# End of a graph layer's second step: the third last tile's sum leaves its accumulator amid the last tile's search for maxima, and the proofs' test stands later

## The chip, the cores and the metric

The kernel runs on one core of one Trainium2 chip. The metric is the device time of one execution in microseconds (us); the median of three runs before the change is 1416.24 us. Engines are called by the names of the profile: PE is TensorE's matmul, PEld its weight load, DVE is VectorE, ACT is ScalarE, POOL is GpSimd, SP is SyncE, which issues most of the DMAs.

## The reference

A graph layer with attention is computed on 3327 nodes of 256 features, in two steps (STEPS = 2). Cut to what matters:

```
def _top_p_attention(X, W1, W2, W3):
    q = X @ W1.T @ W2.T
    k = X @ W3.T
    probs = softmax(q @ k.T, axis=-1)
    idx = argsort(-probs, axis=-1)
    sp = take_along_axis(probs, idx, axis=-1)
    cs = cumsum(sp, axis=-1)
    keep_sorted = cs - sp < 0.9
    mask = zeros(probs.shape, bool).at[rows, idx].set(keep_sorted)
    A = probs * mask
    return A / maximum(A.sum(-1, keepdims=True), 1e-12)

h = maximum(layernorm(x), 0)
R = adj + eye;  R = R / R.sum(-1, keepdims=True)
Z = 0;  Xf = Xa = h
for n in range(2):
    A = _top_p_attention(Xa, W1, W2, W3)
    Xf = R @ Xf
    Xa = A @ Xa
    Z = Z + Xf @ U1[n].T + Xa @ U2[n].T
y = h + Z
out = x + (y - mean(y)) / sqrt(var(y) + 1e-5) * ln_g + ln_b
```

For each row of attention only the largest probabilities are kept, until their sum reaches 0.9. The kernel doesn't sort: it guesses a threshold near the cut, and then finds the exact cut among the values just below the guess.

## The kernel before

The 3327 rows make 26 tiles of 128 rows (NT = 26, numbered 0 to 25). A tile of attention is a block `e` of 128 rows by 3328 columns, in float32. In each of the two steps a tile passes through these stages:

- `weights` (L582): logits on PE, exponentials on ACT, into `e`.
- `measured_twice` (L669, in the second step): passes of ACT over `e` and small operations on DVE and POOL, which guess the threshold.
- `settle` (L725): the exact cut, all on DVE but for one product on POOL. L731 writes the values below the guess into `w`; twenty MAX8 (L736) take the eight largest of each of twenty segments; rounds of MAX8 and MATCH_REPLACE8 (L743, L745) order these candidates; a cumulative sum (L750) gives the cut; L765 masks `e` with it (for the last tile L762 does this in two pieces, of 1024 and of 2304 columns, so that the first columns are ready earlier); L766 makes the factor `ra` that divides by the row's sum; L769 notes one value more for the proof.
- `Sums` (L797): `turn` transposes `e` on PE, four blocks of 128 columns at a time (a part; seven parts to a tile, the last of two blocks), into a buffer `pt` of PSUM, and ACT copies it to `eT` (L812). `sum` multiplies these with the rows of the layer (L824) into the accumulator `pa`. There are two buffers `pt`, three `eT`, and one `pa`. Parts are turned two parts ahead of the sum, so the last parts of one tile's sum stand between turns of the next tile's parts.
- `finish` (L934, in the second step), in pieces that are called one by one: L935 on DVE takes the sum out of `pa`, scales it with `ra` and adds it to `s`; `spread_of` (L458, L459 on DVE) gives mean and variance; the third piece asks SP for the rows `xr` of x (L940, one buffer) and makes 1/sqrt (L465, L466) and `nm` (L943) on POOL; the fourth adds `bet` (L945, POOL) and normalises, by L950 on ACT and L951, L952 on POOL, or by L947, L948 on DVE for the last tile; the fifth stores the rows (L955).

`proof` (L957) ends the second step: `prove(1)` is twelve small DVE instructions (L777 to L788) that test whether all the cuts found are exact, and the second piece adds up the outcome over the partitions with a matmul (`pf`, L961) and writes it to `flag` (L962). All engines read `flag` at the end (L1193); if it were set, a slow search would follow.

The order of the work is written out by hand. In each step a loop over i (L1115) begins the stages of its tiles as generators and then runs through seven slots k (PARTS = 7). In a slot it turns parts, then advances one generator by one piece for each letter of a string, and then sums one part. The strings are in PLAN (L1103) and, for the last rounds of the second step, in LAST (L1106). The letters concerned: `d` is a piece of `settle` of tile i, `n` of `measured` of the tile, `c` what was left of the settling of the tile before, `f` of `finish` of the tile summed last, `s` of the diffusion (`pr`, L911, L1086), `v` of `proof`. In the second step the sum lags four slots (LATE), so that in round i the sum of tile i-2 ends in slot 3 and that of tile i-1 begins in slot 4; `settle` has seven pieces, of which the first ends after L732, the second after ten MAX8, the third after twenty, and the sixth before L769. What is left of a string's generators at the end of a round is run out there (L1174).

The last lines (L1182 to L1185) tie the instructions of PE, ACT, DVE and POOL to the order of this text, each engine for itself. SP's order isn't tied.

Of the kernel before, what the change touches and what calls it, by code (L numbers as in the profile page):

```python
# [22 lines left out]
NT = (N + P - 1) // P  # L23
# [321 lines left out]
def guess_graph_layer(ctx, tc, x, adj, w1t, w2t, w3t, u1t, u2t, ln_g, ln_b, out, flag):  # L345
# [236 lines left out]
    def weights(step, t, live, known=True):  # L582

        r = dict(Z=rec[:, step, 3, t : t + 1])
        qT, r["ms"] = yield from project(step, t, law=known and not step)
        if known and step:
            r["ms"] = law_of(t)
        yield
        r["ms"] = r["ms"] or early.get(t)
        r["e"] = e = es[(2, 3, 0, 1, 4, 5)[t % 6] if step else t % 4]  # L590
        r["za"] = za = small.tile([P, CUT + 1], F32, tag="za", name="za")
        live[step, t] = r
        w = HALF * P
        wd = w // CUT
        for n in range(CUT):
            c = n * wd
            pl = ps_l.tile([P, 2, 512], F32, tag="pl", name="pl")
            for a in range(2):
                p = slice(a * DA, (a + 1) * DA)
                PE.matmul(pl[:, a, :wd], qT[p, :],  # L600
                          keys_of(step, a).rearrange("p a b -> p (a b)")[:, c : c + wd],
                          start=True, stop=True)
            if n < CUT - 1:
                S.activation(e.rearrange("p (a n) -> p a n", a=2)[:, :, c : c + wd], pl[:, :, :wd],  # L604
                             AF.Exp, accum_out=za[:, n : n + 1])
                yield
            else:
                S.activation(e.rearrange("p (a n) -> p a n", a=2)[:, :, c : w - 1], pl[:, :, : wd - 1],
                             AF.Exp, accum_out=za[:, n : n + 1])
                S.activation(e[:, w - 1 : w], pl[:, 0, wd - 1 : wd], AF.Exp, accum_out=za[:, n + 1 :])  # L610
# [108 lines left out]
    def measured(step, r):  # L719
        return measured_twice(r) if step else measured_once(r)  # L720
# [52 lines left out]
    def prove(step):  # L773
        v8, t, tn, Z = (rec[:, step, k, :] for k in range(4))
        ok = small.tile([P, NT], F32, tag="cum", name="ok", bufs=1)
        o2 = small.tile([P, NT], F32, tag="dr", name="o2", bufs=1)
        V.tensor_tensor(ok, v8, t, ALU.is_lt)  # L777
        V.tensor_tensor(o2, tn, t, ALU.is_lt)
        V.tensor_tensor(ok, ok, o2, ALU.mult)
        for a, c, op in ((tn, 0.0, ALU.is_gt), (t, 0.5 * BIG, ALU.is_lt),  # L780
                         (Z, 1.0e-30, ALU.is_gt), (Z, BIG, ALU.is_lt)):
            V.scalar_tensor_tensor(ok, a, c, ok, op, ALU.mult)
        V.tensor_scalar(ok, ok, 0.5, None, ALU.is_lt)
        n = N - (NT - 1) * P
        f = small.tile([P, 1], F32, tag="f", name="f")
        V.tensor_reduce(f, ok[:, : NT - 1], AX.X, ALU.add)
        V.tensor_tensor(fl, fl, f, ALU.add)
        V.tensor_tensor(fl[:n], fl[:n], ok[:n, NT - 1 :], ALU.add)  # L788
        if step == 0:
            V.tensor_scalar(ok, lists[:, :, LIST - 1], 0.0, None, ALU.is_gt)  # L790
            V.scalar_tensor_tensor(ok, ends, float(P), ok, ALU.is_gt, ALU.add)
            V.tensor_reduce(f, ok, AX.X, ALU.add)
            V.tensor_tensor(fl, fl, f, ALU.add)
# [125 lines left out]
    def first_end(t):  # L919
        aT = transposed(live.pop(("r", t)))  # L920
        yield
        pz = ps_r.tile([P, 2 * D], F32, tag="pr", name="pz")
        for c in range(ND):
            PE.matmul(pz, aT[:, c, :], u2[:, c].rearrange("p n d -> p (n d)"), start=c == 0, stop=c == ND - 1)
        S.copy(xw[:, t, :], pz[:, D:])
        sv = row.tile([P, D], F32, tag="sv", name="sv", bufs=2)
        S.copy(sv, pz[:, :D])
        G.tensor_tensor(sv, sv, x0[:, t, :], ALU.add)
        nc.sync.dma_start(sx[t], sv)
        yield  # L930
        yield from prep(aT, t)
# [25 lines left out]
    def proof():  # L957
        prove(1)
        yield
        pf = ps_t.tile([P, 4, P], F32, tag="pt", name="pf")  # L960
        PE.matmul(pf[:1, 0, :1], fl, ones, start=True, stop=True)  # L961
        V.tensor_copy(flag, pf[:1, 0, :1])  # L962

    live, ohs, acs, xgs, done, early = {}, {}, {}, {}, [], {}
    none = iter(())

    def run(work, n=99):
        for _ in range(n):
            next(work, None)
# [133 lines left out]
    PLAN = (("mdsssa", "mdsssa", "edawwp", "msda", "mpdea", "gdawwq", "emdgq"),  # L1103
            ("llcmss", "lnms", "lwwnfd", "lcmdsssg", "fmswqdf", "llmdf", "lmwfd"))

    LAST = {NT - 1: ("cfss", "cn", "ndddddd", "sss", "fsf", "f", "f"), NT: ("cf", "v", "", "", "ff", "f", "fv")}  # L1106
    LATE = (1, 4)
    trace, begin = nc.cur_bb.bb.instructions, len(nc.cur_bb.bb.instructions)
    work = dict(m=none, d=none, f=none)
    later = {}  # L1110
    ordered = []
    for step in range(2):
        sums = Sums(step, live, xw if step else x0, AHEAD[step])

        for i in range(-1, NT + 2):  # L1115
            if step == 0 and i == NT - 3:
                begun = [weights(1, t, live, False) for t in range(3)]
            if step == 1 and i == -1:
                ordered.append(len(trace))
            if step == 1 and i == -1:  # L1120
                run(begun[0])
                prove(0)
                for e in es[4:]:
                    G.memset(e[:, N:NP], 0.0)
            work.update(
                n=work["m"],
                c=work["d"],
                d=settle(step, i, live[step, i]) if valid(i) else none,
                m=measured(step, live[step, i + 1]) if valid(i + 1) else none,
                s=spread(step, i - 2 + 2 * step) if valid(i - 2 + 2 * step) else none,  # L1130
                w=later.pop((step, i + 2), none),
                e=first_end(i - 2) if step == 0 and valid(i - 2) else none,
                a=lister if step == 0 and i else none,
                p=packed(i + 1) if step == 0 and i >= 0 and valid(i + 1) else none,
                g=none if not valid(i + 2 * step) else refetch(i + 2) if step else gathered(i),
                b=none, q=none, v=proof() if step and i == NT else none,
                l=laws(range(3, NT)) if step and i == -1 else none,
            )
            if i >= 0 and valid(i + 3):
                later[step, i + 3] = weights(step, i + 3, live)  # L1140
                work["q"] = itertools.islice(later[step, i + 3], 2 - step)
            if step == 0 and i >= NT - 2 and i < NT + 1:

                work["w"] = itertools.islice(begun[i - NT + 2], CUT - 1)
            if step == 0 and i >= NT - 3 and i < NT:
                work["q"] = itertools.islice(begun[i - NT + 3], 1)
            if i == -1:
                work["w"] = begun[1] if step == 0 else itertools.chain(begun[1], begun[2])
            if step == 0 and i == 0:
                work["w"] = begun[2]  # L1150
            if step == 0 and i < 1:
                work["b"] = itertools.islice(product, MADE if i else NT)
            if step == 1 and i == -1:
                work["g"] = itertools.chain(refetch(0), refetch(1))
            for k in range(PARTS):
                g = PARTS * (i - 1) + k - LATE[step]
                summing = valid(g // PARTS)
                if summing and step:
                    sums.turn(g, min(i, NT - 1))
                for c in "bb" + (LAST.get(i, PLAN[1]) if step else PLAN[0])[k]:  # L1160
                    next(work[c], None)
                if summing and not step:
                    sums.turn(g, min(i, NT - 1))
                if summing:
                    ended = sums.sum(g)
                    if ended and step == 0:
                        live["r", ended[0]] = ended[1]
                    elif ended:
                        work["f"] = finish(ended[0], live.pop(("f", ended[0])), *ended[1])
            if step == 1 and i == -1:  # L1170
                run(work["m"])
            if step == 0 and i == -1:
                G.memset(es[2][:, N:NP], 0.0)
            for c in "lcnwqsepgb" if step else "dmwqsepgb":  # L1174
                run(work[c])
            if step == 0 and i == NT:
                moments(1, gsum)
                for t in range(3):
                    live[1, t]["ms"] = returned(project(1, t, queries=False))
# [50 lines left out]
```

## Time and profile before

| what | us |
|---|---|
| median of three runs | 1416.24 (1415.47 to 1416.34) |
| the profiled execution | 1414.41 |
| its span on the core | 1412.7 |
| what lies around the span in that execution | 1.7 |
| PE busy | 1275.6 (90% of the span) |
| DVE busy | 1220.8 (86%) |
| ACT busy | 1105.4 (78%) |
| POOL busy | 983.1 (70%) |
| last DVE instruction (L948) starts | 1402.98 |
| last store issued (L955) | 1403.49 |

Times inside the span are counted from its start. The span was cut by the profiler into 40 slices of 35 us. In all but the first, the last and those around the middle (where the second step begins) PE and DVE are busy in 90% or more of a slice: there the engines work on several tiles at once. Near the end no tiles are left to fill the gaps. The change lies there, in the last 60 us, and a share of busy time over the whole span says nothing on it; the stretch has to be read by itself. In the timelines an "x8" beside L824 counts records: a matmul in float32 leaves two, so it is four matmuls, one part of a sum.

### The profile page before, as it was taken

Reading aid. Unit: us, or ns where it says so; the run is one execution under the profiler, and the core shown is the slowest. Engines: PE = TensorE matmul, PEld = TensorE weight load, DVE = VectorE, ACT = ScalarE, POOL = GpSimd, SP = SyncE. Lnnn points to the kernel's source line nnn. Section 1 sums busy time; section 2 is a strip of 40 time slices with the busy share of each in tenths; the row PEclk is TensorE's granted clock in tenths of the full one; section 3 lists DMA queues with packets and bytes.
Section 4 is the critical chain, followed back from the end, with each engine's and each line's share of the span. In section 5 each row is a group of like instructions: output and inputs, shape, how many; then the busy total and the mean of one; then the engine's idle time right before and its main releaser. Section 6 shows DMA issues by size and latency. Waiting matters only on the chain.

```text
span 1412.7 us, 22245 instructions
## 1 busy us (share of the span) xinstructions
PE 1275.6 (90%) x6495; PEld 980.1 (69%) x6495; DVE 1220.8 (86%) x3727; ACT 1105.4 (78%) x2423; POOL 983.1 (70%) x1348
## 2 busy tenths in 40 slices
PE   6898999999999999999998479999999999999846
PEld 5545777777777777778786257777777777777745
DVE  6879999999999999998853689999999999999980
ACT  5467887878778787888835689999999999999811
POOL 6214777678667676778853768888888888888721
PEclk9999999999999999999999589999999999999978
DMA  8884454444545454423331211312222122221100
GB/s 273 266 254 127 135 150 130 137 139 141 144 128 147 128 143 144 132 82 91 88 97 49 71 44 54 90 57 79 76 59 87 55 85 59 77 83 53 57 8 22
DMA packets 91203, 149.78 MB, mean 106 GB/s; under 512 B 15265, under 2 KB 58656, under 8 KB 91072
## 3 DMA queue, kind: packets, MB, share of 16 engines
q1 hardware_dynamic: 73616, 105.37, 23.7%
q0 software_dynamic: 16640, 42.69, 11.9%
q8 instruction: 54, 0.88, 0.3%
q14 instruction: 77, 0.63, 0.1%
q10 hardware_dynamic: 816, 0.20, 0.1%
HBM read 120.93 MB, written 27.28 MB: 105 GB/s over the span
## 4 chain that ended last, share of the span: by engine, by line
DVE 51%; PE 25%; ACT 17%; POOL 3%; issue 3%; DMA 1%; SPq 0%; DVEq 0%; POOLq 0%; ACTq 0%
ACT ja L633 11%; PE pa L824 10%; DVE e L765 10%; DVE cand L736 7%; DVE w L731 6%; DVE fm L846 5%; PE pl L600 4%; DVE bb L743 4%; DVE cand L745 4%; PE pt L810 3%; PE pz L988 2%; DVE x L765 2%; ACT eT L812 2%; PE pr L911 1%; ACT e L604 1%
## 5 line engine op out<-in xcount | busy, mean ns | idle before, releaser
L824 PE MATMUL pa<-xw,eT 128*128 128x256 f32 x1352 | 331.1, 387 | 18.6 <-DVE s L935 18.4
L633 ACT ACTIVATE ja<-e,g 128x3328 uint8<-128x3328 f32 x106 | 325.9, 3074 | 0.1
L824 PE MATMUL pa<-x,eT 128*128 128x256 f32 x1352 | 323.7, 381 | 0.0
L824 PEld LDWEIGHTS pa<-xw,eT 128*128 128x128 f32 x1352 | 249.6, 191 | 79.6 <-issue 27.1
L812 ACT COPY eT<-pt 128x512 f32<-128x512 f32 (+1 forms) x364 | 202.1, 556 | 92.9 <-PE pt L810 92.8
L824 PEld LDWEIGHTS pa<-x,eT 128*128 128x128 f32 x1352 | 244.1, 191 | 25.7
L736 DVE MAX8 cand<-w 128x8 f32<-128x168 f32 (+1 forms) x1040 | 251.1, 317 | 0.0
L810 PE MATMUL pt<-ident,e 128*128 128x128 f32 x1144 | 180.6, 278 | 57.9 <-DVE e L765 39.1
L894 POOL DMA_INDIRECT ac<-in_adj,index x130 | 130.2, 1002 | 133.1 <-DVE ms L538 94.9
L903 POOL DMA_INDIRECT xg<-bx,index x130 | 192.4, 1480 | 41.3 <-issue 28.9
L810 PEld LDWEIGHTS pt<-ident,e 128*128 128x128 f32 x1144 | 140.8, 144 | 104.7 <-issue 48.8
L731 DVE SCALAR_TENSOR_TENSOR w<-e,g 128x3328 f32<-128x3328 f32 x44 | 168.9, 3838 | 0.7
L903 POOL DMA_INDIRECT xg<-vx,index x130 | 130.8, 1007 | 45.6 <-issue 33.0
L765 DVE SCALAR_TENSOR_TENSOR e<-e,rec 128x3328 f32<-128x3328 f32 x40 | 156.3, 3907 | 0.7
L911 PE MATMUL pr<-xg,ac 128*128 128x257 f32 (+1 forms) x520 | 139.1, 391 | 11.4 <-DVE s L1086 11.2
L604 ACT ACTIVATE e<-pl 128x832 f32<-128x832 f32 x132 | 112.9, 859 | 36.1 <-PE pl L600 36.0
L911 PEld LDWEIGHTS pr<-xg,ac 128*128 128x128 f32 x520 | 93.9, 195 | 24.9 <-DVE s L1086 11.4
L951 POOL TENSOR_TENSOR s<-s,gam 128x256 f32<-128x256 f32 x25 | 92.5, 3699 | 8.5 <-ACT s L950 8.5
L743 DVE MAX8 bb<-cand 128x8 f32<-128x160 f32 x286 | 92.8, 324 | 6.4
L600 PE MATMUL pl<-after,qT 64*128 64x416 f32 x416 | 96.7, 559 | 0.6 <-ACT qT L528 0.6
L767 POOL TENSOR_TENSOR cum<-dr,bb 128x48 f32<-128x48 f32 x26 | 84.8, 3262 | 15.1 <-DVE rec L755 14.9
L600 PE MATMUL pl<-both,qT 64*128 64x416 f32 x416 | 90.7, 539 | 0.9 <-DVE both L1006 0.9
(259 smaller groups left out, 2197.3 us busy)
## 6 DMA issues: line engine op xcount, KB each, us to landing
at<-in_adj SPq DMA_DIRECT2D x102, 256.0 KB, 3.0
cx<-ac SPq DMA_DIRECT2D x26, 384.0 KB, 2.3
ac<-cx SPq DMA_DIRECT2D x26, 384.0 KB, 3.1
wide<-in_adj SPq DMA_DIRECT2D x10, 832.0 KB, 4.3
e<-in_adj SPq DMA_DIRECT2D x8, 832.0 KB, 5.9
bx<-e SPq DMA_DIRECT2D x26, 128.5 KB, 2.2
own<-bx SPq DMA_DIRECT2D x26, 128.5 KB, 2.9
x<-in_x SPq DMA_DIRECT2D x13, 256.0 KB, 4.7
```

The source lines that it names most:

```text
L600: PE.matmul(pl[:, a, :wd], qT[p, :], keys_of(step, a).rearrange("p a b -> p (a b)")[:, c : c + wd], start=True, stop=True)
L633: S.activation(ja, e, f, bias=guess, scale=sign, accum_out=total)
L731: V.scalar_tensor_tensor(w, e, col(16), e, ALU.is_lt, ALU.mult, accum_out=d2)
L736: V.max(cand[:, 8 * s : 8 * s + 8], w[:, s * SEG : min(NP, (s + 1) * SEG)])
L743: V.max(b8, cand)
L765: V.scalar_tensor_tensor(e, e, at(1), e, ALU.is_ge, ALU.mult, accum_out=ra)
L810: PE.transpose(pt[:, j, :], e[:, (j0 + j) * P : (j0 + j + 1) * P], ident)
L812: S.copy(eT[:, :w, :], pt[:, :w, :])
L824: PE.matmul(self.pa, eT[:, c - 4 * k, :], self.xa[:, j, :], start=c == 0, stop=c == NT - 1)
L894: G.indirect_dma_start(out=ac[:, k, :], out_offset=None, in_=rows, in_offset=bass.IndirectOffsetOnAxis(ap=index[:, t, k : k + 1], axis=0), ...
L903: G.indirect_dma_start(out=xg[:, k, :w], out_offset=None, in_=rows, in_offset=bass.IndirectOffsetOnAxis(ap=index[:, t, k : k + 1], axis=0))
L911: PE.matmul(pr[:, :w], ac[:, k, :], own if k == KT - 1 else xg[:, k, :w], start=k == 0, stop=k == KT - 1)
```

## The change

The strings for the last rounds of the second step are written anew, and there is one more of them (i = NT + 1 = 27, a round that had none of its own). A line is touched so that a proof begun in round 26 is kept for round 27.

```
-    LAST = {NT - 1: ("cfss", "cn", "ndddddd", "sss", "fsf", "f", "f"), NT: ("cf", "v", "", "", "ff", "f", "fv")}
+    LAST = {NT - 1: ("cfss", "cn", "ndd", "sss", "fddddsf", "f", "f"), NT: ("cf", "", "", "", "ff", "fv", "f"),
+            NT + 1: ("fv", "f", "", "", "f", "f", "f")}
...
-                b=none, q=none, v=proof() if step and i == NT else none,
+                b=none, q=none, v=proof() if step and i == NT else work.get("v", none),
```

In round 25, slot 2, two pieces of tile 25's settling remain (up to the tenth MAX8) where there were six; the other four stand in slot 4, behind the first `f`, which is L935 of tile 23. So on DVE L935 of tile 23 moves from behind L766 of tile 25 to between its tenth and eleventh MAX8. The second `f` (L458 and L459 of tile 23) stays where it was, behind L766, and so do the later pieces. On DVE the twelve instructions of `prove(1)` move from ahead of L935 of tile 24 to behind its L459. On PE the matmul `pf` moves behind one further part of tile 25's sum and one further turn. The order on ACT and POOL is the same in both kernels. On SP the reading of `flag` stood between the load of `xr` for tile 24 and the store of tile 24, and stands behind that store and the load of `xr` for tile 25. No instruction is added or taken away on any engine.

## The prediction

> **What bounds the kernel now.** I read the page first: DVE carries 51% of the chain that ended last and PE 25%, but these are means over 1412.7 us, and the change touches only the last 60 us. So I asked for the chain of waits from 1350 us on (columns: start, us, engine, tile, line).
>
> ```profile
> 1354.72 4.67 DVE cand L736 x20
> 1364.85 3.85 DVE e L762 x4
> 1369.51 3.78 PE pa L824 x8
> 1386.11 1.99 PE pa L824 x8
> 1395.13 4.33 PE pa L824 x20
> ```
>
> Until 1369 us the end is set by DVE's settling of tile 25, the last one; after that by PE, which makes two whole sums (tiles 24 and 25) back to back. Why PE starts so late is in the list of waits over 1350 to 1412.7 us (total, times, longest):
>
> ```profile
> PE pa L824 <- DVE s L935: 15.1, 1, 15.1
> ```
>
> PE's timeline shows the place (start, duration; one matmul is two records, so x8 is four blocks of the sum; in brackets the idle time before).
>
> ```profile
> 1353.78 0.60 PE L911 MATMUL pr<-own,ac 128*128 128x256 f32 x2
> 1369.51 3.78 PE L824 MATMUL pa<-xw,eT 128*128 128x256 f32 x8 [15.13 <-DVE s L935]
> 1373.90 1.89 PE L824 MATMUL pa<-xw,eT 128*128 128x256 f32 x8
> 1381.90 0.60 PE L810 MATMUL pt<-ident,e 128*128 128x128 f32 x4
> 1386.11 1.99 PE L824 MATMUL pa<-xw,eT 128*128 128x256 f32 x8
> ```
>
> The sum of tile 23 was complete by 1353.5 us, but `pa` has one buffer, and it is emptied by L935 on DVE, whose turn comes only after all of tile 25's settling. DVE's timeline:
>
> ```profile
> 1354.64 4.75 DVE L736 MAX8 cand<-w 128x8 f32<-128x168 f32 x20
> 1364.85 1.28 DVE L762 SCALAR_TENSOR_TENSOR e<-e,rec 128x1024 f32<-128x1024 f32 x1
> 1368.91 0.16 DVE L766 RECIPROCAL ra<-ra 128x1 f32<-128x1 f32 x1
> 1368.99 0.47 DVE L935 SCALAR_TENSOR_TENSOR s<-pa,ra,s 128x256 f32<-128x256 f32 x1
> 1369.49 0.43 DVE L458 BATCH_NORM_STATS2 st<-s 128x6 f32<-128x256 f32 x1
> 1369.95 0.18 DVE L459 BATCH_NORM_AGGREGATE mv<-st 128x2 f32<-128x6 f32 x1
> ```
>
> L935 wanted nothing but its place in DVE's order for 15 us. Last the order on ScalarE, which becomes decisive below: the finishing step L950 of tile 23 stands between the fifth and the sixth copy of tile 24's turned blocks (the copy at 1374.15 us is the fourth).
>
> ```profile
> 1376.32 0.59 ACT L812 COPY eT<-pt 128x512 f32<-128x512 f32 x1 [1.58 <-PE pt L810]
> 1376.80 0.60 ACT L950 ACTIVATE s<-s,nm,rstd 128x256 f32<-128x256 f32 x1
> 1378.48 0.58 ACT L812 COPY eT<-pt 128x512 f32<-128x512 f32 x1 [1.08 <-PE pt L810]
> ```
>
> And TensorE's granted clock by stretches (third last number of a line):
>
> ```profile
> 1354.00:1369.50 15.50, 0.38 (x2) 0.00 (x0) 14.80 (x52) 0.58 (x1) 1.30 (x1) 0.59 0.00 0
> 1369.50:1374.00 4.50, 4.49 (x13) 3.64 (x14) 3.58 (x15) 0.00 (x0) 1.75 (x4) 0.52 0.00 0
> 1374.00:1386.00 12.00, 11.97 (x67) 10.31 (x65) 0.43 (x1) 3.80 (x7) 1.45 (x2) 1.00 0.07 22
> ```
>
> In stretches of half a microsecond the clock falls to 0.50 at 1356.7, 2.3 us after PE's last work, and is back at 1.00 at 1373.7. So the first 4.2 us of tile 24's sum ran at half speed.
>
> **What the Trainium skill says.** "TensorE: Matmul & The Clock Gate", section "Part 1: The HAM clock gate", says that PE falls to half clock after about an idle window of 3.4 us and needs a busy window of about 3.4 us to come back, the windows free-running. The trace agrees on the two speeds and the grid (from 1356.7 to 1373.7 is 17.0 us, five times 3.4), and shows that a window need not be wholly idle: the one that ended at 1356.7 still held 1.1 us of work, a third. "PSUM — Partial Sum Buffer", section "Engine vs sequencer instructions", says that ScalarE, VectorE and GpSimdE queues are strictly first in, first out, and that matmuls keep program order. The trace agrees: L935 sat behind the settling for 15 us. The sums below rest on both.
>
> **The change part by part.**
>
> 1. L935 of tile 23 goes from behind L766 to the middle of the twenty MAX8. The first ten take 2.36 us from start to next (1331.80 to 1334.16, where the kernel already does this for the tile before), so it starts at 1354.64 + 2.36 = 1357.0 and ends at 1357.47. PE's sum was ready 3.5 us earlier: no wait is added for the ten MAX8 and the settling behind it. It displaces them by 0.39 us (the same L935 in the search before, 1334.16 to 1334.54, and L1086, 1334.91 to 1335.30, are such steps). PE starts tile 24's sum at 1357.5 instead of 1369.5: 12.0 us earlier, after an idle of 3.1 us.
>
> 2. How far PE gets. Up to the first turn of tile 25 stand five parts at 1.73 us (1376.06 to 1377.79), three turns at 0.44 (1375.62 to 1376.06) and the short one at 0.22: 8.65 + 1.32 + 0.22 = 10.2 us at full clock. Before it took 1369.51 to 1381.90 = 12.4 us, so the cold start cost 2.2. At full clock PE is there at 1367.7, and tile 25's first masked columns are ready at 1366.14 + 0.39 = 1366.5.
>
> 3. What is late next. That turn needs a `pt` buffer (there are two), the one that the copy of tile 24's sixth part frees. In ScalarE's order, which the change leaves as it was, this copy stands behind L950 of tile 23. L950 needs `nm` from GpSimd, and that needs L458 and L459 on DVE, which the change leaves behind the whole settling. L766 begins at 1368.91 + 0.39 = 1369.30, L458 at 1369.38 (0.08 after it, as L935 did), L459 ends 0.64 later, as before (1369.49 to 1370.13), at 1370.02; GpSimd's three steps took 1370.13 to 1371.48 = 1.35, so `nm` is there at 1371.37; a hop of 0.07 (as 1377.40 to 1377.47, L950 to L951); L950 holds the queue 0.48 (1376.32 to 1376.80 is such a step), the copy takes 0.58: 1372.51. PE turns tile 25's first part at about 1372.56 against 1381.90, which is 9.34 us earlier. PE stands still for up to 4.9 us before it.
>
> 4. The clock after this standstill. A PE idle for 4.9 us falls to half clock in nearly every position of the 3.4 us grid and stays there until a busy window ends, so half of the cold time is lost: at least half a window, 1.7, at most 3.4 if nearly two windows pass. If PE already went cold in the gap of 3.1 us, its first parts run longer, at the expense of the standstill only, which may then be too short to count: loss 0. I take 1.8 (the page's window halved, little more; the trace's own case was 2.2), ends 0 and 3.4.
>
> 5. What follows is the old tail: L935 of tile 24 between the sums, sum of tile 25, L935 to L948, last store; 1386.11 to 1412.7, moved as a block. L950 of tile 24 had 3.2 us to spare (`nm` at 1388.06, L950 at 1391.28) and keeps them, as its chain starts at the same L935. xr for tile 24 is loaded behind tile 23's store: L951 and L952 end near 1373.7, the load is issued at about 1374.1, and L945 wants it after tile 24's L459, at about 1380.
>
> 6. The proof: twelve DVE instructions, 1370.69 to 1373.46 = 2.8 us, go behind tile 24's L459, where DVE was idle (4.13 us before L962). They end near 1382.2; `pf`, moved one part later on PE, comes at 1393.03 - 7.5 = 1385.5, so 3.3 us hide it; without this cover the excess would stand on PE. The matmul costs 0.12 on PE in either place (1390.64 to 1390.76). On SP the flag's load moves behind tile 24's store and the next xr load; only the last store, 10 us later, stands behind it: nothing.
>
> Sum: 9.34 - 1.8 = 7.5 us off the span of 1412.7, so 1405.2. What lies around the span (1414.41 - 1412.7 = 1.7) stays. The timed median is 1.8 above the profiled run; the same gain gives 1416.24 - 7.5 = 1408.7.
>
> **Rivals.** (a) The clock is kept, or PE goes cold in the first gap and has recovered by 1372.6: gain 9.3, 1406.9. For it: gaps of 2.5 us (before 1334.68) left the clock alone; against: 4.9 us is long, and the gap of 6.1 us before 811 us was followed by half clock. (b) L950 doesn't bind, because its chain runs earlier than I read it: PE goes through at 1367.7, gain 14.2, 1402.0. Against: the order on DVE and ScalarE is fixed by hand, and L458 keeps its place. (c) The wait only moves: something in the tail that I hold to be covered (the xr load, the proof, tile 24's L950) is late by over 6.5 us; then less than 2.8 us, 0.2%, remains, about what a measurement can tell from no change: 1415. Against: the margins of 3 us and more above. (d) Slower: PE, restarted at 1372.6, doesn't recover its clock and runs the rest of both sums, 17.5 us at full clock (1381.90 to 1399.45), at half. That costs 17.5 against 9.3 gained: 1424.4. It decides from 18.7 us of cold running on; the longest cold work seen, with gaps in it, is 795.9 to 803.6, 7.7 us.
>
> **How the numbers follow.** Forecast 0.62, (a) 0.24, (b) 0.05, (c) 0.05, (d) 0.04. Faster: 0.62 + 0.24 + 0.05 = 0.91; same 0.05; slower 0.04. The range takes (a) with 0.7 us for the unknown grid position in the runs before (their own cold loss may be 1.7 to 3.4 where the profiled one had 2.2), and the largest cold loss (gain 5.9, 1410.3) with a little over: 1406.2 to 1410.6.
>
> **What would show it.** L935 of tile 23 at 1357.0 amid the MAX8; PE's idle split in two, about 3 us ended by L935 and up to 5 us ended by ScalarE's copy behind L950; the first turn of tile 25 near 1372.6; the clock at 0.50 for 3 to 5 us after it; L935 of tile 24 near 1378, the last sum's end near 1392, the span near 1405. The prediction is wrong if L950 of tile 23 runs before 1370 us (then b), if PE's second gap is missing, or if the last sum's start moves by less than 5 us.

## The result, and the profile after

| | before | after |
|---|---|---|
| median, us | 1415.86 (4 runs, 1414.3 to 1416.34) | 1406.62 (4 runs, 1406.2 to 1408.79) |
| ratio after / before | | 0.9938, 95% interval 0.9926 to 0.9949 |
| profiled execution, us | 1414.41 | 1408.79 |
| its span, us | 1412.7 | 1407.1 |
| tile 25's L731 starts, us | 1350.78 | 1352.80 |
| first MAX8 of tile 25's search, us | 1354.64 | 1356.66 |
| from that MAX8 to the end of the span, us | 58.06 | 50.44 |

The change makes the kernel faster by 9.2 us, or 7.2 to 10.5 by the interval. The two profiled spans differ by less, 5.6 us, because in the execution profiled after the change everything ahead of the changed place came 2.0 us late. The order of instructions there is the same in both kernels, so the place for a comparison is the stretch from tile 25's search on: it is 7.62 us shorter.

The list of waits from 1345 us on, kernel after (total, times, longest):

```profile
ACT s L950 <- POOL nm L943: 8.6, 1, 8.6
...
PE pt L810 <- ACT eT L812: 4.6, 1, 4.6
...
PE pa L824 <- DVE s L935: 3.1, 1, 3.1
```

The one wait of 15.1 us has split in two. The accumulator now holds PE for 3.1 us. Then, five parts of the sum later, a copy on ScalarE holds it for 4.6, and that copy was held by L950, which itself waited 8.6 us for `nm`. DVE's timeline shows the moved instruction and what stayed behind:

```profile
1356.66 2.44 DVE L736 MAX8 cand<-w 128x8 f32<-128x168 f32 x10
1359.01 0.47 DVE L935 SCALAR_TENSOR_TENSOR s<-pa,ra,s 128x256 f32<-128x256 f32 x1
1359.40 2.40 DVE L736 MAX8 cand<-w 128x8 f32<-128x168 f32 x10
...
1371.33 0.16 DVE L766 RECIPROCAL ra<-ra 128x1 f32<-128x1 f32 x1
1371.41 0.41 DVE L458 BATCH_NORM_STATS2 st<-s 128x6 f32<-128x256 f32 x1
1371.86 0.18 DVE L459 BATCH_NORM_AGGREGATE mv<-st 128x2 f32<-128x6 f32 x1
```

The statistics L458 and L459 of the same tile still come after all of the settling. GpSimd makes `nm` from them, L950 needs it, and the copies queue behind L950 (ScalarE's timeline; the last line holds two copies, of the sixth and seventh parts):

```profile
1364.23 0.59 ACT L812 COPY eT<-pt 128x512 f32<-128x512 f32 x1 [1.58 <-PE pt L810]
1373.42 0.60 ACT L950 ACTIVATE s<-s,nm,rstd 128x256 f32<-128x256 f32 x1 [8.60 <-POOL nm L943]
1373.92 0.84 ACT L812 COPY eT<-pt 128x512 f32<-128x512 f32 x2
```

PE's timeline shows both standstills, and what the second leaves behind: the first turn takes 1.04 us instead of 0.60 and the part behind it 3.23 instead of 1.89.

```profile
1359.54 1.99 PE L824 MATMUL pa<-xw,eT 128*128 128x256 f32 x8 [3.15 <-DVE s L935]
...
1374.54 1.04 PE L810 MATMUL pt<-ident,e 128*128 128x128 f32 x4 [4.56 <-ACT eT L812]
1375.37 3.23 PE L824 MATMUL pa<-xw,eT 128*128 128x256 f32 x8
...
1380.48 1.99 PE L824 MATMUL pa<-xw,eT 128*128 128x256 f32 x8
```

The granted clock (third last number) in the stretches before, at and after that place:

```profile
1361.00:1374.50 13.50, 8.98 (x49) 7.55 (x47) 10.90 (x35) 2.26 (x5) 3.46 (x6) 1.00 0.00 0
1374.50:1378.50 4.00, 3.96 (x13) 3.32 (x14) 0.00 (x0) 0.85 (x2) 1.04 (x2) 0.57 0.20 66
1378.50:1393.80 15.30, 15.16 (x81) 12.71 (x79) 3.60 (x15) 3.80 (x7) 3.21 (x6) 1.00 0.08 20
```

### The profile page after: what moved, and what is told of

Same layout as the page of the kernel before. It is cut to its first block, busy times and chain, and to the rows that moved or that the text cites. A ratio compares the mean times of both kernels' runs of the same rounds, so it can differ in the third digit from the quotient of the medians.

```text
span 1407.1 us, 22248 instructions
## 1 busy us (share of the span) xinstructions
PE 1278.7 (91%) x6495; PEld 980.9 (70%) x6495; DVE 1220.4 (87%) x3727; ACT 1105.6 (79%) x2423; POOL 989.7 (70%) x1348
## 4 chain that ended last, share of the span: by engine, by line
DVE 51%; PE 24%; ACT 17%; POOL 3%; issue 3%; DMA 1%; DVEq 0%; SPq 0%; POOLq 0%; ACTq 0%
ACT ja L633 11%; DVE e L765 10%; PE pa L824 9%; DVE cand L736 7%; DVE w L731 6%; DVE fm L846 5%; PE pl L600 4%; DVE bb L743 4%; DVE cand L745 4%; PE pt L810 3%; PE pz L988 2%; DVE x L765 2%; ACT eT L812 2%; PE pr L911 1%; ACT e L604 1%
## 5 line engine op out<-in xcount | busy, mean ns | idle before, releaser
L903 POOL DMA_INDIRECT xg<-bx,index x130 | 184.8, 1421 | 41.0 <-issue 30.0
L731 DVE SCALAR_TENSOR_TENSOR w<-e,g 128x3328 f32<-128x3328 f32 x44 | 169.1, 3842 | 0.7
L767 POOL TENSOR_TENSOR cum<-dr,bb 128x48 f32<-128x48 f32 x26 | 84.9, 3264 | 15.5 <-DVE rec L755 15.3
```

Source lines behind the costliest of these rows:

```text
L731: V.scalar_tensor_tensor(w, e, col(16), e, ALU.is_lt, ALU.mult, accum_out=d2)
L903: G.indirect_dma_start(out=xg[:, k, :w], out_offset=None, in_=rows, in_offset=bass.IndirectOffsetOnAxis(ap=index[:, t, k : k + 1], axis=0))
```

## The experiments

In what follows "L731 to the end" is the time from the start of tile 25's L731 to the end of the profiled span; it leaves out the scatter ahead of it. Each kernel was timed beside the kernel before on the same chip, and ratios are to that. The ten runs (`after_again` is the changed kernel once more) were measured in three groups (l935_only, proof_only, stats_early, kept_warm; after_again, kept_warm_24, stats_nm_early, all_earlier; gap1_filled, both_filled), in which the kernel before had medians of 1415.51, 1414.39 and 1415.41 us; times of different groups aren't set against each other directly.

| kernel | median, us | ratio to before, 95% interval | L731 to the end, us | clock at half, us of the span |
|---|---|---|---|---|
| before (profile) | | | 61.92 | 1356.7 to 1373.7 |
| changed kernel (profile) | | | 54.3 | 1374.7 to 1378.2 |
| l935_only | 1405.73 | 0.9937 (0.9923 to 0.995) | 52.53 | 1357.7 to 1361.2 |
| proof_only | 1415.54 | 1.0 (0.9992 to 1.0008) | 61.95 | 1357.2 to 1374.5 |
| stats_early | 1406.9 | 0.9933 (0.9919 to 0.9946) | 53.74 | 1374.7 to 1378.0 |
| kept_warm | 1406.93 | 0.9938 (0.9925 to 0.9952) | 53.42 | 1358.2 to 1361.7 |
| after_again | 1407.43 | 0.9945 (0.9932 to 0.9959) | 54.83 | L731 to 1353.4, 1370.5 to 1377.2 |
| kept_warm_24 | 1406.59 | 0.9948 (0.9934 to 0.9961) | 52.58 | 1357.7 to 1361.0 |
| stats_nm_early | 1402.58 | 0.9916 (0.9902 to 0.9929) | 49.35 | 1358.5 to 1362.0 |
| all_earlier | 1400.64 | 0.9902 (0.9887 to 0.9917) | 47.4 | none |
| gap1_filled | 1406.93 | 0.9942 (0.9928 to 0.9956) | 53.9 | 1371.7 to 1375.2 |
| both_filled | 1406.24 | 0.9934 (0.992 to 0.9947) | 52.62 | none |

The last column lists the half clock between tile 25's L731 and the last matmul; the ends are read in quarters of a microsecond.

**The two parts of the change alone.** In `l935_only` the proof stands where it stood before:

```
-    LAST = {..., NT: ("cf", "", "", "", "ff", "fv", "f"),
-            NT + 1: ("fv", "f", "", "", "f", "f", "f")}
+    LAST = {..., NT: ("cf", "v", "", "", "ff", "f", "fv")}
```

> L935 of tile 23 amid the search for maxima as in the changed kernel, the proof at its old place. Theory: the whole gain comes from L935, so the time equals the changed kernel's, 9 us (0.65%) under before within the spread of the timed runs, and in the trace tile 24's L935 again starts about 23 us after the first MAX8 of tile 25's search (23.3 in the changed kernel, 30.9 before). Rival: the proof's twelve DVE instructions, 2.8 us, held the last tiles back; then this kernel is about 2.8 us slower than the changed one.

In `proof_only` L935 stands where it stood before, and the proof at its new place:

```
-    LAST = {NT - 1: ("cfss", "cn", "ndd", "sss", "fddddsf", "f", "f"), ...
+    LAST = {NT - 1: ("cfss", "cn", "ndddddd", "sss", "fsf", "f", "f"), ...
```

> The proof at its new place, L935 of tile 23 at its old one, behind the whole settling. Theory: the proof was hidden in DVE's idle time before and after, so the time equals that of the kernel before within 1 us (ratio 1.000). Rival (the proof held the tail back): 2.8 us faster than before.

The two ratios settle it: L935 alone gives all of the gain, and the proof's place is worth nothing that can be measured (L731 to the end 61.95 against 61.92). But `l935_only` took 52.53 us from L731 to the end, 1.8 less than the changed kernel's profile, which the proof cannot explain. Its PE timeline does:

```profile
1358.00 3.52 PE L824 MATMUL pa<-xw,eT 128*128 128x256 f32 x8 [3.14 <-DVE s L935]
...
1372.99 0.66 PE L810 MATMUL pt<-ident,e 128*128 128x128 f32 x4 [3.04 <-ACT eT L812]
1373.49 1.89 PE L824 MATMUL pa<-xw,eT 128*128 128x256 f32 x8
```

Here it was the first gap that tripped the clock, that is, after which it fell to half (the first part took 3.52 us instead of 1.99). PE came later to the place where it waits for ScalarE, so the second gap was only 3.04 us, and this time what followed ran at full speed. The loss fell into time in which PE would have stood still anyway.

**What holds PE the second time.** `stats_early` puts L458 and L459 of tile 23 right behind its L935:

```
-    LAST = {NT - 1: ("cfss", "cn", "ndd", "sss", "fddddsf", "f", "f"), ...
+    LAST = {NT - 1: ("cfss", "cn", "ndd", "sss", "ffdddds", "f", "f"), ...
```

> The changed kernel with L458 and L459 of tile 23 right behind its L935. GpSimd's L465 to L943 still stand behind its L767 of tile 25. Theory (L950 of tile 23, late by its statistics, holds the sixth copy on ScalarE, and that copy holds PE): nm comes some 3.5 us earlier, as soon as L767 is done (L767 ended at 1368.68 in the changed kernel's trace, so nm at about 1370.0 instead of 1373.4), the second standstill of PE shrinks from 4.6 to about 1 us, the clock stays at 1.00 after it; 3.4 us of standstill and 1.7 of cold clock gone, about 4 to 5 us faster than the changed kernel, 1402. Rival (PE waits for tile 25's mask or for something else at this place): no faster than the changed kernel.

That missed: the ratio is that of the changed kernel, PE's second standstill was still 4.04 us and still ended by ScalarE's copy, and L950 started 20.09 us after L731 in place of 20.62. The statistics were ready 12 us earlier, and yet `nm` was not. GpSimd's timeline:

```profile
1367.90 1.31 POOL L767 TENSOR_TENSOR cum<-dr,bb 128x48 f32<-128x48 f32 x1 [16.01 <-DVE rec L755]
1369.29 2.41 POOL L465 TENSOR_SCALAR rstd<-mv 128x1 f32<-128x1 f32 x1
1371.78 0.57 POOL L466 TENSOR_TENSOR rstd<-rstd,half 128x1 f32<-128x1 f32 x1
```

L465, an operation on one column that takes 0.22 to 0.25 us for the other tiles of this step (0.51 for tile 25, beside DVE's L947), took 2.41. It ended at 1371.70, when DVE had just finished the second piece of L762:

```profile
1369.00 2.62 DVE L762 SCALAR_TENSOR_TENSOR e<-e,rec 128x2304 f32<-128x2304 f32 x1
1371.55 0.08 DVE L762 DVE_READ_ACCUMULATOR e<-e,rec 128x1 f32 x1
```

The Trainium skill, "SBUF — State Buffer", section "SBUF: two separate sides", describes this: DVE and GpSimd share a pair of ports as an exclusive lock, and a DVE operation with two SBUF inputs (L762 multiplies `e` with its own comparison) and a GpSimd operation that reads SBUF block each other for the whole instruction. The trace agrees with its 2.41 against 0.23 us. The profile of before had shown it already: there L767 took 1.30 us beside the first piece of L762, and 0.27 for the tile before, with DVE idle.

So `stats_nm_early` also puts the third piece of `finish` forward: on GpSimd L465 to L943 then stand ahead of tile 25's L767, and so ahead of L762:

```
+    LAST = {NT - 1: ("cfss", "cn", "ndd", "sss", "fffdddds", "", "f"), ...
```

> The changed kernel with L458, L459 of tile 23 right behind its L935, and with GpSimd's L465 to L943 ahead of its L767 of tile 25, so that they run before DVE's L762. Theory (L950 of tile 23 is held by nm, and in stats_early nm was held because a GpSimd operation does not proceed while DVE's L762 runs: L465 took 2.41 us there, to the end of L762, against 0.23): L465 takes 0.2 to 0.3 us again, nm is there about 2 us after L935, L950 of tile 23 runs near 12 us after tile 25's L731 in place of 20.6, the second standstill of PE goes, tile 24's L935 starts about 20.6 us after L731 (up to 3.4 more if PE goes cold in the first gap) in place of 27.2, and the time is 4 to 5 us under the changed kernel's, 1401 to 1403. Rival (PE is held by tile 25's mask or by GpSimd in another way): no more than 1 us gained.

The time came as expected, and L465 took 0.23 us again. GpSimd:

```profile
1359.50 0.23 POOL L465 TENSOR_SCALAR rstd<-mv 128x1 f32<-128x1 f32 x1 [8.23 <-DVE mv L459]
...
1360.48 0.26 POOL L943 TENSOR_SCALAR nm<-mv,rstd 128x1 f32<-128x1 f32 x1
```

L950 started 13.4 us after L731 (about 12 were expected), right behind the copy ahead of it, the second standstill is gone from PE's timeline, and tile 24's L935 started at 22.2 us although PE had gone cold in its first gap. The median is 4.9 us under `after_again` on the same chip (1402.58 against 1407.43). With that it is shown that L950's place, behind late statistics, was the next limit.

`all_earlier` goes one step further and puts L935, L458 and L459 ahead of the first MAX8:

```
+    LAST = {NT - 1: ("cfss", "cn", "nd", "sss", "fffddddds", "", "f"), ...
```

> As stats_nm_early, but L935, L458 and L459 of tile 23 stand ahead of the first MAX8 of tile 25's search, right behind L732. Theory: L935 starts about 3.9 us after L731 (PE's sum is ready at 2.7), PE's first gap shrinks from 3.1 to about 0.8 us and cannot trip the clock; the first turn of tile 25 then waits for its mask (about 16.4 us after L731), tile 24's L935 starts at about 20.1, and the time is 0.5 to 2 us under that of stats_nm_early, about 1400.5. Rival (one more microsecond on DVE ahead of the mask costs more than the gap): slower than stats_nm_early by up to 1 us.

PE's timeline has only two short gaps left, and the second is ended by tile 25's mask, so DVE's settling bounds the end again:

```profile
1355.79 1.99 PE L824 MATMUL pa<-xw,eT 128*128 128x256 f32 x8 [0.79 <-DVE s L935]
...
1367.97 0.63 PE L810 MATMUL pt<-ident,e 128*128 128x128 f32 x4 [1.74 <-DVE e L762]
```

From 1300 us on the clock never fell before the last matmul. The median of 1400.64 is the lowest of all: 6.8 us under the changed kernel on the same chip, ratio 0.9902 to the kernel before. It beats both kernels.

**What the standstills cost in clock.** `kept_warm` and `kept_warm_24` put 36 and 24 transposes that nobody uses into the second gap:

```
+                if step and i == NT and k == 2:
+                    pw = ps_l.tile([P, 2, 512], F32, tag="pl", name="pw")
+                    for _ in range(36):
+                        PE.transpose(pw[:, 0, :P], ident, ident)
```

> The changed kernel with 36 additional transposes of the identity into a free PSUM buffer, put on PE between the fifth part of tile 24's sum and the first turn of tile 25; at 0.11 us each they fill 3.9 of the 4.6 us of PE's second standstill and are used by nobody. Theory (the standstill costs 1.7 us of half clock after it): the clock stays at 1.00, and from the first turn of tile 25 to the start of its sum it takes 4.2 us instead of 5.9; the span from the first MAX8 of tile 25's search falls from 50.4 to about 48.7 us, the time by up to 1.7 us. Rival (what follows the standstill was slow for another reason, or the added work delays the turn): not faster, or up to 4 us slower.

> As kept_warm, with 24 additional transposes in place of 36: 2.6 us at 0.11 us each, so that they end before ScalarE's copy releases PE even where the first gap made PE slow (with 36 they ran 0.9 us over). Theory: the clock stays at 1.00 after the second gap wherever the grid lies, about 52.5 us from tile 25's L731 to the end of the span; the time is the changed kernel's or up to 1.7 us less. Rival (the half clock is not what the idle time costs): 54.3 us from L731 to the end.

Neither tells the theories apart. In both profiled executions PE went cold (to half clock) in the first gap already, as in `l935_only`, where the second gap did no harm without any transposes, and no time was gained. In `kept_warm` the 36 transposes outlasted the shortened gap: the first turn of tile 25 came 22.6 us after L731 (1373.20 - 1350.58) where it was 21.7 in the changed kernel. The repeated profile of the changed kernel, `after_again`, was a second cold case:

> The changed kernel once more, beside the three others, for its time on this chip and for a second profile. Theory (a free-running grid of 3.4 us decides which gap of PE trips the clock): either PE goes to half clock in the first gap (3.1 us) and is back at 1.00 after the second, then about 52.5 us from tile 25's L731 to the end of the span, or it goes there in the second gap, then 54.3; nothing beyond these by more than 1.7 us. Rival (the clock after the second gap is a fixed cost): 54.3 again. Time 1405.5 to 1408.8.

Its 54.83 us lie near the longer of the two lengths, 2.3 us above the 52.53 of `l935_only`. Half clock up to 1353.4 had drawn out PE's work here, so that the first gap was only 1.5 us and did not trip the clock; the second, of 4.56, did. So the first gap had to be controlled too. `gap1_filled` puts 22 transposes into the first gap, `both_filled` 36 more into the second:

```
+                fill = {(NT - 1, 4): 22, (NT, 2): 36}.get((i, k), 0) if step else 0
```

(with 0 in place of 36 in `gap1_filled`).

> The changed kernel with 22 additional transposes of the identity, used by nobody, in PE's first gap (2.4 of its 3.1 us, ahead of tile 24's sum), so that the clock cannot fall there and the second gap keeps its full 4.6 us. Theory (idle time of PE costs half clock by the 3.4 us grid): the second gap then always trips the clock, 54.2 to 55.5 us from tile 25's L731 to the end of the span, time 1407 to 1408.5. Rival (the two lengths seen, 52.5 and 54.3 to 54.8, come from something other than the first gap's clock): 52.5 is as likely as before.

> As gap1_filled, with 36 more transposes in the second gap (3.9 of its 4.6 us). Theory: the clock is 1.00 from tile 25's L731 to the last sum, 52.5 us from L731 to the end of the span in every position of the grid, about 2 us under gap1_filled. Rival (the clock is not what costs these 2 us, or the additional work delays PE): no faster than gap1_filled.

PE's timelines behind the second gap, first `gap1_filled`:

```profile
1372.33 1.11 PE L810 MATMUL pt<-ident,e 128*128 128x128 f32 x4 [4.56 <-ACT eT L812]
1373.24 2.83 PE L824 MATMUL pa<-xw,eT 128*128 128x256 f32 x8
```

and `both_filled`:

```profile
1375.41 0.66 PE L810 MATMUL pt<-ident,e 128*128 128x128 f32 x4 [0.64 <-ACT eT L812]
1375.91 1.89 PE L824 MATMUL pa<-xw,eT 128*128 128x256 f32 x8
```

The waiting instruction is released at the same distance from L731 in both (21.73 us). With PE idle before it, the part behind takes 2.83 us, with PE busy 1.89, and L731 to the end falls from 53.9 to 52.62. So the standstill's clock costs time, here 1.3 us, less than the 1.7 that I had as the least and than the 2 expected between these two runs. In the medians the difference is 0.7 us with intervals that overlap, so the timed runs alone don't show it.

**Which gap trips the clock.** The clock records of the twelve traces answer this. In each of them every beginning and every end of half clock lies on one grid of 3.41 us, and the grid lies differently to the work from one execution to the next. From 1300 us to the last matmul there are, in the twelve together, 287 whole stretches of the grid at full clock. After 15 of them the clock fell, and in these PE was busy for at most 40% of the stretch; after the other 272 it stayed, and there PE was busy for 41% or more. So it matters how the grid cuts a gap. In the windows below, set on the grid, the number behind the length is PE's busy time. In `l935_only` nearly all of the first gap lies in one stretch, and the clock fell at its end:

```profile
1354.29:1357.70 3.41, 0.57 (x4) 0.17 (x2) 3.37 (x14) 0.58 (x1) 0.00 (x0) 1.00 0.00 0
```

In the changed kernel's profile the same gap is cut in two, and the clock stayed:

```profile
1354.18:1357.60 3.42, 2.21 (x13) 1.60 (x11) 3.38 (x7) 0.59 (x1) 0.00 (x0) 1.00 0.00 0
1357.60:1361.01 3.41, 1.47 (x7) 1.32 (x8) 3.41 (x15) 0.00 (x0) 0.00 (x0) 1.00 0.00 0
```

Earlier in the span the border is less sharp: the clock also fell after fuller stretches, near 770 us after some with PE busy up to 68%.

## Why the prediction was right

The forecast was 1408.7 us in a range of 1406.2 to 1410.6; measured were 1406.62. By its own steps, after against before, each counted from the first MAX8 of tile 25's search:

1. L935: predicted 2.36 us after the first MAX8, measured 2.35 (1359.01 - 1356.66), displacing the search by 0.39 as predicted. Tile 24's sum starts 2.88 us after that MAX8 in place of 14.87: 12.0 earlier, as predicted.
2. PE was at tile 25's first turn after five parts, at about 1369.8 by its last part's start and the 1.73 of a part, 10.3 us after the sum's start against 10.2.
3. The wait for L950 and the copy: the first turn at 17.88 us (1374.54 - 1356.66) against a predicted 17.92 (1372.56 - 1354.64). This chain over four engines, read from the order and from single durations, held to 0.04 us; `stats_nm_early` shows that it was the cause.
4. The clock: 1.73 us lost in the profiled execution (5.94 from the first turn to the sum of tile 25, where it was 4.21 before), 1.8 predicted.
5. The old tail moved as a block: from the start of tile 25's sum to the end 26.6 us (1407.1 - 1380.48) as before (1412.7 - 1386.11).
6. The proof ran in DVE's idle time, 1381.03 to 1383.78, and `pf` came 3.4 us later, where 3.3 were predicted; `proof_only` shows that its place costs nothing.

The sum, 7.5 us, stands against 7.62 in this stretch of the profile. The median fell by 9.2, which lies nearer to rival (a), 9.3. The path and the waits were right; the term that I sized wrongly is the fourth. A single figure of 1.8 us stood for something that differs from execution to execution with the place of the grid: the two profiles of the changed kernel lost 1.7 and 2.3 us (`after_again`), `gap1_filled` 1.3, and `l935_only`, which differs only in the proof, nothing behind its second gap. So forecast and rival (a) both occur, and that the one profile after the change came within 0.1 us of 1.8 was luck. I may also have given the first gap too little weight, as one way to rival (a) only: it tripped the clock in four of the six profiles in which it was 3.1 us long. The kernel before stands still for 15 us at this place, and lost its share in its own profile and in that of `proof_only`. How often each case falls among the timed runs cannot be read from times, since the rest of the kernel scatters more: over the twelve profiles tile 25's L731 started between 1350.58 and 1353.68 us. What makes that scatter is left open; one piece is visible in the profile after, half clock from 1337.2 to 1340.7, after a gap that did not trip the clock in the profile before. The interval of 7.2 to 10.5 us holds both figures.

Rival (b), a gain of 14.2 with L950 not binding, didn't occur, but it named what was still to be had: `all_earlier` has it nearly, 14.5 us less from L731 to the end than before. Rival (c) is excluded by steps 5 and 6. Rival (d), a clock that doesn't recover, was not seen: the longest half clock after the second gap was 6.7 us (`after_again`), where 18.7 were needed.

## What to carry to other kernels

An instruction that frees a buffer belongs at the point where its input is ready, not where its engine has finished something else; but follow the rest of its chain too, because the wait goes to the next instruction that stayed behind in an in-order queue. If a chain crosses GpSimd, look at what DVE runs at that moment, not only at GpSimd's own queue. Where PE stands still, compare over a stretch that begins after the scatter, and over more than one profile, before a microsecond or two is put down to the change.

## What the runs showed of the hardware that was not expected

- A GpSimd operation on one column took 2.41 us while DVE masked a tile, and 0.23 for the same tile ahead of that mask; it undid a move that the order of instructions alone made look right.
- The same gap of PE may trip the clock or not, by how the grid of 3.41 us cuts it (the border in these last 100 us was between 40% and 41% of a stretch busy): gaps of 3.1 us did in `l935_only`, `kept_warm`, `kept_warm_24` and `stats_nm_early`, and did not in the changed kernel's first profile nor in `stats_early`; one of 2.5 us before tile 23's sum did in the changed kernel and not before the change.
- An earlier loss of clock can be free, or even useful: in `l935_only` the first gap slowed PE, the second shrank to 3.04 us and, cut in two by the grid (PE busy 2.02 and 1.77 us of 3.41), did not slow what followed, and that execution was shorter by 1.8 us from L731 on than the changed kernel's profile.
